# Graph attention and a transformer block: the first groups' work and the last groups' projection in another order

## The chip, the cores and the metric

The kernel runs on one core of a Trainium2 chip. The metric is device time in microseconds (us) of one execution, the median of several runs; lower is better. The engines have short names here: PE is TensorE's matrix multiply, PEld its weight load, DVE VectorE, ACT ScalarE, POOL GpSimd, and SP SyncE, which here only issues transfers (DMAs). Each engine works through its own list of instructions in order and waits for the others by semaphores.

## The reference

There are 64 batches of 64 tokens with 256 features, all float32. A graph attention comes first, then a transformer block with conditioning (cond) by batch:

```python
# graph attention, on x (B, N, F) = (64, 64, 256), with kv the first 20 tokens
q_exp = where(x.sum(-1) == 0, 0, cond)            # by row
self_feat = concat([x, q_exp]) @ W_self.T + b_self
output = self_feat
for d in range(2):
    A = (adj if d == 0 else swapaxes(adj, 1, 2))[:, :, :20, :]      # 11 labels
    mask, label_bias = A.sum(-1) > 0, A @ w_bias + b_bias
    aff = einsum('bnhd,bmhd->bnhm', q, k) / sqrt(16)                # 16 heads
    w = softmax(where(mask, aff, NEG) + label_bias)
    output = output + einsum(w, kv) through Wout + bout
x = x + relu(output)
# transformer block
shift, scale, gate (twice) = split(silu(cond) @ Wt + bt, 6)
h = layernorm(x) * g1 + be1;  h = h * (1 + scale_msa) + shift_msa
x = x + gate_msa * (attention(h) @ Wproj + bproj)
h = layernorm(x) * g2 + be2;  h = h * (1 + scale_mlp) + shift_mlp
x = x + gate_mlp * (gelu(h @ W1 + b1) @ W2 + b2)
```

## The kernel before

**Groups and tiles.** The batches go in nine groups, NB = [4, 8, 8, 8, 8, 8, 8, 8, 4] (L26). A group of 8 is 512 tokens, four tiles of 128 tokens (two batches a tile); the first and the last group have two tiles. Features lie on the partitions (xT, sfT, hT: 128 x 2 x tokens), so that the weights are the stationary operand and 512 tokens stream past them.

**The order is written by hand** (`tc.manual_schedule()`, L71): every engine's list is in the order of the calls in the source. `start()` (L945) does group 0's graph attention, most of group 1's, and the first two slots; then a loop over g = 1 to 7 runs `boundary(g)` and `period(g)`; `finish()` (L1059) does the rest. In period g, the transformer attention of group g, the graph attention of group g+1 and the MLP of group g-1 go side by side. A `slot` (L723) takes one tile of each: scores on PE, then the softmax on DVE, ACT and POOL, transposes back on PE, and the output products. Places named "p", "f0", "f1", "d0", "f2", "f2b", "d1", "d2", "f3" in the slot take further calls from lists of fills, chiefly to give PE work while a softmax is under way.

**PSUM.** Four banks rotate (`bank`, L89); one can be held for a long sum. Two pairs of banks, pa and pb, take the scores. A call that takes a bank waits until whoever read the bank's last content is done.

**Steps of the graph attention.** `graph_k` (L395, keys kT, with wk), `graph_keys` (L425, keys spread by head into kblk; on POOL, for group 1 on ACT in four instructions), `graph_q` (L412, with wq), `graph_scores` (L443), `graph_masked` (L461, DVE times keep, POOL plus term), `graph_exp` (L472: maximum and difference on DVE, exponential on ACT), `graph_normal` (L479: sum and reciprocal on DVE, product w<-w,sm on POOL), `graph_turned` (L486, transposes pwT, ACT copies wT), `graph_output` (L498, po; then ACT, and POOL adds to xT). keep and term come from the adjacency in seven steps (`mask_step`, L334, DVE), six that read it and a last one. `nonzero_rows` (L271) and `row_pairs` (L292) prepare the test for zero rows (pz).

**Steps of the block.** `norm_tokens` (L524, transposes pxT, ACT copies xn), `norm_stats` (L533, DVE statistics and POOL power rstd), `normed` (L544, DVE), `modulated` (L552, transposes phT, DVE times amp, POOL plus off). `half_normed` (L845) is these four as steps 0 to 3 for the first two tiles. Then `block_qk` (pqk), `block_keys` (kb, POOL), `block_scores`, `block_exp` (DVE, ACT), `block_normal` (DVE, POOL), `block_turned` (ppT), `block_attended` (pao), and `block_proj` (L676): four matmuls over the whole group, DVE adds the bias and multiplies by the gate, POOL adds to xT. The MLP is `mlp_up` (pu; Gelu on ACT), `mlp_down` (py), `mlp_gated`, `mlp_out` (store).

**Time projections** (L236) make gate, amp and off from silu(cond): t = 0 to 5, shift, scale and gate for either half; `time_added` (L247) evacuates them on DVE. amp2 and off2 need t = 3 and 4, gate 2 and 5.

**Loads.** SP issues nearly all loads; the first are, in order, xT of group 0, w_self, adj and adj_t of group 0 (L143), wk[0] and wk[1] (L144), then xT of group 1, wout and the rest. ACT issues cond, the other half of w_self, vecs and wq; POOL some broadcasts. `graph_k(0, d)` needs wk[d] and kv; the masks of group 0 need adj and adj_t.

**The end.** `finish()` has E3 (the last tile of group 7, called m), E0 and E1 (the two tiles of group 8, z), the MLP's second half of group 6 (l), the projection and second normalising of m (K[0], K[1]: two tiles each), and the MLPs of m and z. `block_proj(m, c)` needs all four tiles of m attended.

Of the kernel before, what the change touches and what calls it, by code (L numbers as in the profile page):

```python
# [9 lines left out]
F32 = mybir.dt.float32  # L10
I32 = mybir.dt.int32
AF = mybir.ActivationFunctionType
ALU = mybir.AluOpType
# [4 lines left out]
P = 128  # L18
# [28 lines left out]
def graph_attention_then_dit_block(  # L47
# [33 lines left out]
    def unit(name):  # L81

        return gp.tile([P, 512], F32, tag="u", name=name, bufs=8)
# [35 lines left out]
    def load_adj(g):  # L119
        G = groups[g]  # L120
        G.adj = []
        for src in (adj[ds(G.t0, G.T), 0 : M * L], adj_t[ds(G.t0, G.T), :]):
            if g == 0:
                a_d = unit("a_0")[:, 0 : G.nt * M * L].bitcast(I32).rearrange("p (j c) -> p j c", j=G.nt)
            else:
                a_d = two.tile([P, NT, M * L], I32, tag="a_d", name="a_d")[:, 0 : G.nt]
            nc.sync.dma_start(a_d, src.rearrange("(j p) c -> p j c", p=P))
            G.adj.append(a_d)

    def load_w(name, src, k, n, eng):  # L130
        t = wpool.tile([P, k, n], F32, tag=name, name=name)
        eng.dma_start(t, src.rearrange("(k p) n -> p k n", p=P))
        return t
# [8 lines left out]
    w_self_sb = load_w("w_self", w_self[0:D], 2, D, nc.sync)  # L142
    load_adj(0)  # L143
    wk_sb = [load_w(f"wk{d}", wk[d], 2, D, nc.sync) for d in range(2)]  # L144
# [89 lines left out]
    pt_of = {}  # L234

# [440 lines left out]
    def block_proj(g, c):  # L676
        G = groups[g]
        py = bank("pproj")[:, 0 : G.T]
        for k in range(2):
            nc.tensor.matmul(py, wproj_sb[:, k, ts(c, P)], G.aoT[:, k, 0 : G.T], start=(k == 0), stop=(k == 1))  # L680
        if c == 0:
            G.yT = []
        yT = two.tile([P, GT], F32, tag="tq", name="yT") if g == NG - 1 else unit("yT")
        G.yT.append(yT[:, 0 : G.T])
        gated(G.yT[c], py, "bproj", 0, g, c)
        nc.gpsimd.tensor_tensor(G.xT[:, c, :], G.xT[:, c, :], G.yT[c], ALU.add)

# [35 lines left out]
    def slot(e, c, e_next, c_next, before, fill):  # L723
# [4 lines left out]
        C = graph_scores(*c, sc) if c else None  # L728
        if Eb:
            block_turned(Eb)  # L730
        elif Cb:
            graph_turned(Cb[0])
# [137 lines left out]
    def period(g):  # L870
# [4 lines left out]
        def up(*ms):  # L875
            return [(mlp_up, m, i) for i in ms]
# [60 lines left out]
        if n == NG - 1:  # L937

            fills = fills[:3]
            fills[2]["f3"] = up(6) + next_(half_normed, 0) + up(7) + next_(half_normed, 1)  # L940
# [4 lines left out]
    def start():  # L945
# [71 lines left out]
        for t in t1:  # L1017
            graph_masked(t)
        graph_v(1, 0)
# [3 lines left out]
        block_keys(0, 0)  # L1023
        graph_v_spread(1)
# [7 lines left out]
        graph_keys(1, 2)  # L1032
        graph_exp(t1[0])
# [3 lines left out]
        row_pairs(2)  # L1037
        fills = [
            {
                "f0": [(nonzero_rows, 2)],  # L1040
# [6 lines left out]
                    (time_projection, 2), (half_normed, 1, 0), (mask_step, 2, 3), (time_projection, 3),  # L1047
# [5 lines left out]
                "d0": [(half_normed, 1, 2)],  # L1053
                "f3": [(time_projection, 4), (half_normed, 1, 3), (time_projection, 5)],
# [4 lines left out]
    def finish(before):  # L1059

        z, m, l = NG - 1, NG - 2, NG - 3
        Z, A = groups[z], groups[m]
        E3 = block_scores(m, 3, [pair("pa", "sca"), pair("pb", "scb")])
        block_turned(before[0])
        block_exp(E3)
        mlp_down(l, 0, 6, 7)
        half_normed(z, 2)
        block_attended(before[0], pair("pa", "pao")[:, 0])
        mlp_gated(l, 0)
        mlp_out(l, 0)  # L1070
        mlp_down(l, 1, 0)
        half_normed(z, 3)
        block_normal(E3)
        mlp_down(l, 1, 1, 2)
# [3 lines left out]
        mlp_down(l, 1, 3)  # L1078
        block_turned(E3)
        block_qk(z, 0, 0)  # L1080
        block_qk(z, 0, 1)
        block_keys(z, 1)
        block_attended(E3, bank("pao"))
        E0 = block_scores(z, 0, [pair("pa", "sca"), pair("pb", "scb")])
        block_exp(E0)
        block_proj(m, 0)
        block_proj(m, 1)
        block_v(z, 0)
        E1 = block_scores(z, 1, [pair("pa", "sca"), pair("pb", "scb")])
        block_exp(E1)  # L1090
        mlp_down(l, 1, 4)
        K = [Tile() for _ in range(A.nt // 2)]
        norm_tokens(K[0], A.xT, 0)
        norm_stats(K[0])
        mlp_down(l, 1, 5)
        norm_tokens(K[1], A.xT, 1)
        block_normal(E0)
        norm_stats(K[1])
        normed(K[0])
        mlp_down(l, 1, 6)  # L1100
        A.h2T = gp.tile([P, 2, GT], F32, tag="h2b", name="h2T")
        modulated(K[0], A.h2T, 0, amp2, off2, m)
        block_turned(E0)
        normed(K[1])
        block_normal(E1)
        mlp_down(l, 1, 7)
        block_attended(E0, pair("pa", "pao")[:, 0])
        modulated(K[1], A.h2T, 1, amp2, off2, m)
        mlp_gated(l, 1)
        mlp_out(l, 1)  # L1110
        mlp_up(m, 0)
        block_turned(E1)
        mlp_up(m, 1)
        block_attended(E1, pair("pb", "pao")[:, 0])
        block_proj(z, 0)
        block_proj(z, 1)
        mlp_up(m, 2)
        mlp_down(m, 0, 0)
        k = Tile()
        mlp_up(m, 3)  # L1120
        norm_tokens(k, Z.xT, 0)
        norm_stats(k)
        for i in range(4, 6):
            mlp_up(m, i)
            mlp_down(m, 0, i - 3)
        normed(k)
        Z.h2T = new_hT("hT")
        mlp_up(m, 6)
        mlp_down(m, 0, 3)
        modulated(k, Z.h2T, 0, amp2, off2, z)  # L1130
        mlp_up(m, 7)
        mlp_down(m, 0, *range(4, 8))
# [80 lines left out]
```

## Time and profile before

| | us |
|---|---|
| median of 3 runs (708.24, 708.87, 710.34) | 708.87 |
| the profiled execution itself | 706.65 |
| its span, first to last instruction | 704.9 |
| PE busy | 666.8 |
| DVE busy | 494.0 |
| POOL busy | 373.8 |
| ACT busy | 353.8 |

The mean clock granted to PE was 0.985. The costliest groups are the two MLP products, py (L705) with 121.6 us in 288 records and pu (L695) with 109.3 in 256; a float32 matmul shows as two records. Among the others, the average POOL product of `block_normal` (128x1024) takes 1.90 us, that of `graph_normal` 1.36, and the DVE difference of `graph_exp` (L476) 1.60.

The page has the busy time of the engines, then the span in 40 slices of 17.6 us with the busy share in tenths, the chain of work that ended last, and groups by line. Waits are listed as "who line <- whom: us in total, times, longest". A timeline line has the start, the duration, the engine, line and operation, the shape and how many follow each other, and in brackets how long the engine had been idle and what ended that.

### The profile page before, as it was taken

The page shows a single profiled execution, that of the slowest core. Times are in us where ns is not written, and L with a number is a line of the kernel's source. Part 1 is how long each engine was busy: PE and PEld are TensorE (multiplying, and loading weights), DVE is VectorE, ACT ScalarE, POOL GpSimd, SP SyncE. Part 2 cuts the span into 40 slices and gives each one's busy share as a digit, 9 for nine tenths or more (in the row PEclk, how much of TensorE's full clock was granted, in tenths as well). Part 3 has the DMA queues.
Part 4 walks back from the last instruction along what each step waited for, and adds up shares of the span by engine and source line. Part 5 has one row for each costly group of instructions (what it writes and reads, how often), then busy time and mean ns, then how long its engine had stood idle before and what let it go on. Part 6 is the DMA issues. An engine that isn't in the chain of part 4 may idle for free.

```text
span 704.9 us, 15418 instructions
## 1 busy us (share of the span) xinstructions
PE 666.8 (95%) x6414; PEld 408.8 (58%) x6414; DVE 494.0 (70%) x847; ACT 353.8 (50%) x627; POOL 373.8 (53%) x372
## 2 busy tenths in 40 slices
PE   6997889899999999999999999999999999996897
PEld 6664655676655655555655655555655656464446
DVE  3688866789777867887787967887777867557111
ACT  2345333773367435754377535654377537653312
POOL 5545335764676546844575546844665565444310
PEclk8998999999999999999999999999999999998999
DMA  8425040003100040003100040003000100000000
GB/s 282 137 70 185 2 132 18 17 23 95 50 16 17 20 145 17 1 32 103 47 17 16 21 146 16 2 31 93 3 8 12 37 4 2 2 16 1 16 15 31
DMA packets 34382, 33.42 MB, mean 47 GB/s; under 512 B 5608, under 2 KB 28200, under 8 KB 34312
## 3 DMA queue, kind: packets, MB, share of 16 engines
q1 hardware_dynamic: 32808, 31.22, 14.0%
q8 instruction: 51, 0.84, 0.6%
q10 hardware_dynamic: 1232, 0.88, 0.4%
q0 software_dynamic: 272, 0.33, 0.2%
q14 instruction: 19, 0.16, 0.1%
HBM read 25.59 MB, written 6.83 MB: 46 GB/s over the span
## 4 chain that ended last, share of the span: by engine, by line
PE 81%; DVE 10%; ACT 4%; POOL 2%; DMA 2%; issue 1%; ACTq 0%; POOLq 0%; DVEq 0%
PE pu L695 14%; PE py L705 14%; PE pqT L418 8%; PE pqk L576 7%; PE ppT L644 4%; PE pv L584 4%; PE pwT L492 3%; PE pproj L680 3%; PE pf L320 3%; PE pk L403 3%; PE po L510 2%; PE pv L367 2%; PE pao L655 2%; PE sca L614 2%; PE phT L556 2%; PE pxT L529 2%
## 5 line engine op out<-in xcount | busy, mean ns | idle before, releaser
L705 PE MATMUL py<-u,w 128*128 128x512 f32 (+1 forms) x288 | 121.6, 552 | 0.2 <-ACT u L697 0.2
L695 PE MATMUL pu<-h2T,w 128*128 128x512 f32 (+1 forms) x256 | 109.3, 570 | 3.1 <-POOL h2T L563 2.5
L470 POOL TENSOR_TENSOR w<-w,term 128x640 f32<-128x640 f32 x32 | 49.4, 1547 | 72.2 <-DVE w L465 40.2
L695 PEld LDWEIGHTS pu<-h2T,w 128*128 128x128 f32 x256 | 47.4, 190 | 50.1 <-issue 43.1
L705 PEld LDWEIGHTS py<-u,w 128*128 128x128 f32 x288 | 51.2, 191 | 37.7 <-issue 34.4
L637 POOL TENSOR_TENSOR pr<-pr,sm 128x1024 f32<-128x1024 f32 x32 | 60.9, 1902 | 23.0 <-DVE sm L636 20.5
L477 ACT ACTIVATE w<-w 128x640 f32<-128x640 f32 x32 | 23.5, 736 | 87.1 <-DVE w L476 87.1
L521 POOL TENSOR_TENSOR xT<-xT,sfT 128x256 f32<-128x256 f32 x32 | 23.8, 743 | 79.1 <-ACT sfT L520 53.8
L418 PE MATMUL pqT<-sfT,wq 128*128 128x512 f32 (+1 forms) x144 | 61.7, 557 | 0.0
L576 PE MATMUL pqk<-hT,wqkv 128*128 128x512 f32 (+1 forms) x144 | 59.7, 552 | 0.7 <-POOL hT L563 0.6
L697 ACT ACTIVATE u<-pu,vec 128x512 f32<-128x512 f32 (+1 forms) x72 | 42.9, 640 | 34.1 <-PE pu L695 33.2
L484 POOL TENSOR_TENSOR w<-w,sm 128x640 f32<-128x640 f32 x32 | 43.4, 1360 | 29.1 <-DVE sm L483 29.1
L625 DVE TENSOR_REDUCE mx<-sca 128x8 f32<-128x512 f32 x32 | 22.0, 688 | 52.0 <-PE sca L454 43.8
L538 DVE BATCH_NORM_STATS2 st<-xn 128x6 f32<-128x256 f32 x64 | 26.1, 408 | 39.8 <-ACT xn L531 39.8
L635 DVE TENSOR_REDUCE sm<-pr 128x16 f32<-128x1024 f32 x32 | 38.9, 1216 | 20.9 <-ACT pr L631 19.9
L542 POOL TENSOR_TENSOR rstd<-rstd,mhalf 128x2 f32<-128x2 f32 x32 | 23.4, 731 | 55.1 <-DVE rstd L541 54.4
L476 DVE TENSOR_TENSOR w<-w,mx 128x640 f32<-128x640 f32 x32 | 51.2, 1601 | 1.1
L419 ACT ACTIVATE qT<-pqT,vec 128x512 f32<-128x512 f32 (+1 forms) x36 | 23.0, 640 | 52.2 <-PE pqT L418 52.2
L647 ACT COPY pT<-ppT 128x512 f32<-128x512 f32 x64 | 34.5, 591 | 28.8 <-PE ppT L644 28.8
L577 ACT ACTIVATE qk<-pqk,vec 128x512 f32<-128x512 f32 (+1 forms) x36 | 23.1, 640 | 47.3 <-PE pqk L576 47.3
L631 ACT ACTIVATE pr<-pr 128x1024 f32<-128x1024 f32 x32 | 33.8, 1057 | 25.7 <-DVE pr L627 25.5
L547 DVE TENSOR_SCALAR xn<-xn,mv,rstd 128x256 f32<-128x256 f32 x64 | 40.1, 668 | 5.2 <-POOL rstd L542 5.2
(140 smaller groups left out, 1439.2 us busy)
## 6 DMA issues: line engine op xcount, KB each, us to landing
xT<-in_x_t SPq DMA_DIRECT2D x7, 512.0 KB
out<-xT SPq DMA_DIRECT2D x14, 256.0 KB
a_d<-in_adj SPq DMA_DIRECT2D x7, 440.0 KB
a_d<-in_adj_t SPq DMA_DIRECT2D x7, 440.0 KB
x_g<-in_x SPq DMA_DIRECT2D x5, 512.0 KB
vblk<-vd SPq DMA_DIRECT2D x28, 80.0 KB
w<-in_w SPq DMA_DIRECT2D x2, 1024.0 KB
vd<-v_sb SPq DMA_DIRECT2D x7, 256.0 KB
```

The costliest lines, as they stand in the source:

```text
L418: nc.tensor.matmul(pq, wq_sb[d][:, k, ts(c, P)], G.sfT[:, k, :], start=(k == 0), stop=(k == 1))
L470: nc.gpsimd.tensor_tensor(t.w, t.w, G.term[:, :, j, :].unsqueeze(1).to_broadcast([P, H, 2, M]), ALU.add)
L476: nc.vector.tensor_tensor(wf, wf, mx.unsqueeze(2).to_broadcast([P, 2 * H, M]), ALU.subtract)
L484: nc.gpsimd.tensor_tensor(wf, wf, sm.unsqueeze(2).to_broadcast([P, 2 * H, M]), ALU.mult)
L547: nc.vector.tensor_scalar(key.xn[:, i, :], key.xn[:, i, :], key.mv[:, i, 0:1], key.rstd[:, i : i + 1], ALU.subtract, ALU.mult,)
L576: nc.tensor.matmul(pp, wqkv_sb[:, k, ds(i * D + c * P, P)], G.hT[:, k, 0 : G.T], start=(k == 0), stop=(k == 1))
L635: nc.vector.tensor_reduce(sm, t.pr, AX.X, ALU.add)
L637: nc.gpsimd.tensor_tensor(t.pr, t.pr, sm.unsqueeze(2).to_broadcast([P, H, N]), ALU.mult)
L647: nc.scalar.copy(t.pT[:, ts(q4, 4), :], pt.rearrange("p (i t) -> p i t", i=4))
L695: nc.tensor.matmul(pu, w1_sb[:, k, ts(m, P)], G.h2T[:, k, 0 : G.T], start=(k == 0), stop=(k == 1))
L697: nc.scalar.activation(G.u[m], pu, AF.Gelu, bias=col("b1", m))
L705: nc.tensor.matmul(G.py, w2_sb[:, m, ts(c, P)], G.u[m], start=(m == 0), stop=(m == 7))
```

## The change

It touches the two ends of the program and leaves `boundary` as it is; of the periods only the last one's third slot changes.

At the start:
- wk[0] and wk[1] are loaded ahead of group 0's adjacency.
- The keys of group 1's third tile (`graph_keys(1, 2)`) are issued right after the masks of its first two, ahead of ACT's four qk evacuations; the first exponential stands between two and two of these, the second behind them.
- `row_pairs(2)` stands ahead of the two `graph_normal`.
- A new place "p2" in `slot`, behind the scores and ahead of the transposes, takes time projection 2, which was in the first slot's "f3".
- In the second slot, step 2 of `half_normed(1)` moves from "d0" to "d1"; time projection 4 moves behind step 3, and its evacuation behind that of time projection 5.

At the end a new `pair_proj(g, j2)` projects two tiles (256 tokens): eight matmuls of four 128x128 blocks into one bank, two DVE instructions, one POOL add. It replaces both calls of `block_proj` for m (as two pairs) and for z (as one). The first pair of m goes into the third slot of the last period, ahead of up(7). In `finish`, the normalising of K[0] is spread ahead of E3's output, K[1]'s follows the second pair's projection, three up products of m stand before E1's transposes.

```diff
     w_self_sb = load_w("w_self", w_self[0:D], 2, D, nc.sync)
+    wk_sb = [load_w(f"wk{d}", wk[d], 2, D, nc.sync) for d in range(2)]
     load_adj(0)
-    wk_sb = [load_w(f"wk{d}", wk[d], 2, D, nc.sync) for d in range(2)]
...
+    def time_product(t):
+        time_projection(t, bank("pt"))
...
-        yT = two.tile([P, GT], F32, tag="tq", name="yT") if g == NG - 1 else unit("yT")
-        G.yT.append(yT[:, 0 : G.T])
+        G.yT.append(unit("yT")[:, 0 : G.T])
...
+    def pair_proj(g, j2):
+
+        G = groups[g]
+        py = bank("pproj").rearrange("p (c t) -> p c t", c=2)
+        t2 = ts(j2, 2 * P)
+        for c in range(2):
+            for k in range(2):
+                nc.tensor.matmul(
+                    py[:, c], wproj_sb[:, k, ts(c, P)], G.aoT[:, k, t2], start=(k == 0), stop=(k == 1)
+                )
+        y = two.tile([P, GT], F32, tag="tq", name="y").rearrange("p (c t) -> p c t", c=2)
+        b4 = ds(G.b0 + 4 * j2, 4)
+        for c in range(2):
+            nc.vector.scalar_tensor_tensor(
+                y[:, c].rearrange("p (b n) -> p b n", n=N), py[:, c].rearrange("p (b n) -> p b n", n=N),
+                col("bproj", c), gate[:, c, b4].unsqueeze(2).to_broadcast([P, 4, N]), ALU.add, ALU.mult,
+            )
+        nc.gpsimd.tensor_tensor(G.xT[:, :, t2], G.xT[:, :, t2], y, ALU.add)
...
         C = graph_scores(*c, sc) if c else None
+        fill("p2")
         if Eb:
...
-            fills[2]["f3"] = up(6) + next_(half_normed, 0) + up(7) + next_(half_normed, 1)
+            fills[2]["f3"] = up(6) + next_(half_normed, 0) + [(pair_proj, g, 0)] + up(7) + next_(half_normed, 1)
...
             graph_masked(t)
+        graph_keys(1, 2)
         graph_v(1, 0)
         graph_v(1, 1)
         block_qk(0, 1, 0)
         block_qk(0, 1, 1)
         block_keys(0, 0)
+        graph_exp(t1[0])
         graph_v_spread(1)
...
         block_qk(0, 0, 0)
         block_qk(0, 0, 1)
-        graph_keys(1, 2)
-        graph_exp(t1[0])
+        row_pairs(2)
         graph_exp(t1[1])
         graph_normal(t1[0])
         graph_normal(t1[1])
-        row_pairs(2)
         fills = [
             {
+                "p2": [(time_projection, 2)],
...
-                    (time_projection, 2), (half_normed, 1, 0), (mask_step, 2, 3), (time_projection, 3),
+                    (half_normed, 1, 0), (mask_step, 2, 3), (time_projection, 3),
...
-                "d0": [(half_normed, 1, 2)],
-                "f3": [(time_projection, 4), (half_normed, 1, 3), (time_projection, 5)],
+                "d1": [(half_normed, 1, 2)],
+                "f3": [(half_normed, 1, 3), (time_product, 4), (time_projection, 5), (time_added, 4)],
```

`finish` after the change, from its beginning to the last `modulated`; the rest is as before:

```python
E3 = block_scores(m, 3, [pair("pa", "sca"), pair("pb", "scb")])
block_turned(before[0]); half_normed(z, 2); block_exp(E3); mlp_down(l, 0, 6, 7)
block_attended(before[0], pair("pa", "pao")[:, 0]); mlp_gated(l, 0); mlp_out(l, 0)
half_normed(z, 3); norm_tokens(K[0], A.xT, 0); mlp_down(l, 1, 0)
block_normal(E3); norm_stats(K[0]); mlp_down(l, 1, 1)
block_qk(z, 1, 0); block_qk(z, 1, 1); block_keys(z, 0); mlp_down(l, 1, 2)
block_turned(E3); block_qk(z, 0, 0); block_qk(z, 0, 1)
normed(K[0]); block_keys(z, 1); modulated(K[0], A.h2T, 0, amp2, off2, m)
block_attended(E3, bank("pao"))
E0 = block_scores(z, 0, [pair("pa", "sca"), pair("pb", "scb")])
block_exp(E0); mlp_down(l, 1, 3); pair_proj(m, 1); block_v(z, 0); block_normal(E0)
E1 = block_scores(z, 1, [pair("pa", "sca"), pair("pb", "scb")])
mlp_down(l, 1, 4); norm_tokens(K[1], A.xT, 1); norm_stats(K[1]); mlp_down(l, 1, 5, 6)
normed(K[1]); block_turned(E0); modulated(K[1], A.h2T, 1, amp2, off2, m)
block_exp(E1); mlp_down(l, 1, 7); block_attended(E0, bank("pao"))
mlp_gated(l, 1); mlp_out(l, 1); mlp_up(m, 0); block_normal(E1); mlp_up(m, 1); mlp_up(m, 2)
block_turned(E1); mlp_down(m, 0, 0); mlp_up(m, 3)
block_attended(E1, pair("pb", "pao")[:, 0]); mlp_down(m, 0, 1); pair_proj(z, 0)
mlp_up(m, 4); mlp_down(m, 0, 2); mlp_up(m, 5); norm_tokens(K[2], Z.xT, 0); norm_stats(K[2])
mlp_down(m, 0, 3); mlp_up(m, 6); normed(K[2]); mlp_down(m, 0, 4); mlp_up(m, 7)
modulated(K[2], Z.h2T, 0, amp2, off2, z)
```

More of the change, by code (lines that the diff above doesn't have):

```diff
@@ L1062, in finish @@
         Z, A = groups[z], groups[m]
+        K = [Tile() for _ in range(3)]
+        A.h2T = gp.tile([P, 2, GT], F32, tag="h2b", name="h2T")
         E3 = block_scores(m, 3, [pair("pa", "sca"), pair("pb", "scb")])
         block_turned(before[0])
+        half_normed(z, 2)
         block_exp(E3)
         mlp_down(l, 0, 6, 7)
-        half_normed(z, 2)
         block_attended(before[0], pair("pa", "pao")[:, 0])
@@ L1070, in finish @@
         mlp_out(l, 0)
+        half_normed(z, 3)
+        norm_tokens(K[0], A.xT, 0)
         mlp_down(l, 1, 0)
-        half_normed(z, 3)
         block_normal(E3)
-        mlp_down(l, 1, 1, 2)
+        norm_stats(K[0])
+        mlp_down(l, 1, 1)
         block_qk(z, 1, 0)
@@ L1077, in finish @@
         block_keys(z, 0)
-        mlp_down(l, 1, 3)
+        mlp_down(l, 1, 2)
         block_turned(E3)
@@ L1081, in finish @@
         block_qk(z, 0, 1)
+        normed(K[0])
         block_keys(z, 1)
+        modulated(K[0], A.h2T, 0, amp2, off2, m)
         block_attended(E3, bank("pao"))
@@ L1085, in finish @@
         block_exp(E0)
-        block_proj(m, 0)
-        block_proj(m, 1)
+        mlp_down(l, 1, 3)
+        pair_proj(m, 1)
         block_v(z, 0)
+        block_normal(E0)
         E1 = block_scores(z, 1, [pair("pa", "sca"), pair("pb", "scb")])
-        block_exp(E1)
[L1091 to L1105, printed above, removed]
+        mlp_down(l, 1, 4)
+        norm_tokens(K[1], A.xT, 1)
+        norm_stats(K[1])
+        mlp_down(l, 1, 5, 6)
+        normed(K[1])
+        block_turned(E0)
+        modulated(K[1], A.h2T, 1, amp2, off2, m)
+        block_exp(E1)
         mlp_down(l, 1, 7)
-        block_attended(E0, pair("pa", "pao")[:, 0])
-        modulated(K[1], A.h2T, 1, amp2, off2, m)
+        block_attended(E0, bank("pao"))
         mlp_gated(l, 1)
@@ L1111, in finish @@
         mlp_up(m, 0)
+        block_normal(E1)
+        mlp_up(m, 1)
+        mlp_up(m, 2)
         block_turned(E1)
-        mlp_up(m, 1)
+        mlp_down(m, 0, 0)
+        mlp_up(m, 3)
         block_attended(E1, pair("pb", "pao")[:, 0])
[L1115 to L1126, printed above, removed]
-        Z.h2T = new_hT("hT")
[L1128 to L1132, printed above, removed]
+        mlp_down(m, 0, 1)
+        pair_proj(z, 0)
+        mlp_up(m, 4)
+        mlp_down(m, 0, 2)
+        mlp_up(m, 5)
+        norm_tokens(K[2], Z.xT, 0)
+        norm_stats(K[2])
+        mlp_down(m, 0, 3)
+        mlp_up(m, 6)
+        normed(K[2])
+        mlp_down(m, 0, 4)
+        mlp_up(m, 7)
+        Z.h2T = new_hT("hT")
+        modulated(K[2], Z.h2T, 0, amp2, off2, z)
+        mlp_down(m, 0, 5, 6, 7)
         mlp_gated(m, 0)
```

## The prediction

> **What bounds the kernel now.** I read the page first, then the waits of TensorE, its timeline round the longest ones, one-microsecond windows there for the clock, and last the ScalarE timeline at 51 to 62 us. Page and waits:
>
> ```profile
> PE 666.8 (95%) x6414; PEld 408.8 (58%) x6414; DVE 494.0 (70%) x847; ACT 353.8 (50%) x627; POOL 373.8 (53%) x372
> ...
> PE   6997889899999999999999999999999999996897
> ...
> PEclk8998999999999999999999999999999999998999
> ```
>
> ```profile
> PE phT L556 <- DVE xn L547: 8.9, 6, 6.0
> PE pk L403 <- DMA wk<-in_wk: 4.6, 1, 4.6
> PE pwT L492 <- POOL w L484: 3.3, 2, 2.5
> PE pu L695 <- POOL h2T L563: 2.5, 1, 2.5
> ...
> PE ppT L644 <- DVE hT L559: 2.0, 1, 2.0
> ```
>
> TensorE is the bound: 666.8 of 704.9 us busy, so 38 us without work, and the slices put that at the two ends (slices 1 to 8 and 37 to 40). The middle, periods 1 to 6, which the change doesn't touch, has 9s. The waits name the holes, the timeline dates them:
>
> ```profile
> 13.13 3.67 PE L403 MATMUL pk<-kv,wk 128*128 128x80 f32 x16 [4.57 <-DMA wk<-in_wk]
> ```
>
> ```profile
> 646.32 1.14 PE L556 MATMUL phT<-ident,xn 128*128 128x128 f32 x4 [6.01 <-DVE xn L547]
> 647.25 1.91 PE L644 MATMUL ppT<-ident,pr 128*128 128x128 f32 x8
> ...
> 654.09 1.98 PE L695 MATMUL pu<-h2T,w 128*128 128x512 f32 x4 [2.55 <-POOL h2T L563]
> ```
>
> The windows add a second cost. Columns: stretch, its length, busy us of PE, PEld, DVE, ACT, POOL, then the granted clock, DMA share and GB/s.
>
> ```profile
> 12.00:13.00 1.00, 0.00 (x0) 0.00 (x0) 0.93 (x3) 0.00 (x0) 0.00 (x0) 0.50 1.06 386
> ```
>
> ```profile
> 60.00:61.00 1.00, 0.23 (x2) 0.00 (x0) 1.00 (x4) 0.73 (x2) 1.00 (x1) 0.50 0.94 365
> ...
> 65.00:66.00 1.00, 1.00 (x2) 0.45 (x2) 1.00 (x1) 0.00 (x0) 0.63 (x1) 0.50 0.05 17
> 66.00:67.00 1.00, 1.00 (x16) 0.61 (x17) 0.84 (x2) 0.59 (x1) 0.00 (x0) 0.97 0.00 0
> ```
>
> After each long hole the clock is half: from 11.4 to 18.3, 59.2 to 66.1 and 642.9 to 649.7, 6.8 us each. Half of TensorE's busy time inside is lost where TensorE is the bound: 2.6 (13.13 to 18.3), up to 2.9 (5.86 busy) and 1.7 us (646.3 to 649.7). The hole at 56.2 to 58.6 comes from ScalarE's order:
>
> ```profile
> 54.03 1.37 ACT L432 ACTIVATE kblk<-kT,hmask 128x160 f32<-128x160 f32 x4
> 55.30 1.35 ACT L477 ACTIVATE w<-w 128x640 f32<-128x640 f32 x2
> ```
>
> The two exponentials of group 1 stand behind four projections and the third tile's keys, and behind them come sums, reciprocals (DVE to 58.3) and the two normalisings (POOL, from 57.41).
>
> [...] the drops lie 14 and 171 windows of 3.413 us apart. One window with 1.0 us of work dropped, one with 1.6 (90.0 to 93.4) did not, one with 2.45 stayed at half. [...] L476 takes 0.83 to 2.02 us here[...]. [...] Here adj landed by 8.3, adj_t at 11.5 and wk[0] at 13.0 us.
>
> **Part 1, wk ahead of the adjacency (SP).** Four transfers swap; bytes, lane waits and everything behind stay. wk[0] takes adj's place (262 KB for 225), so it should land before 9.4; wk[1] takes adj_t's, 11.5 to 12.0. Then pk waits for kv (POOL, 10.87) and starts at 10.9 instead of 13.13: 2.2. pk and pqT took 7.95 us, partly at half clock. At full clock they are 2.0 + 3.45 us (16 records of 0.215, half a row of L418), with about 0.25 for wk[1]; wq landed at 12.0 and 13.4 by what SP's issues waited for, in time. That saves 2.25. Scores start at 16.6 for 21.05: 4.4. Cover: adj_t now lands where wk[1] did, by 15.0 (pk ran through then). Three mask steps of 0.61 and 0.7 for keep and term end at 17.6; scores end at 17.9. Each us later than 15.3 would cost one. No absolute arrival binds behind it: wt, wqkv and xT are in by 22 us.
>
> **Part 2, keys, exponentials and first time projection.** The third keys need only kT and a free kblk (scores of tile 0, 46.7), so ScalarE does them at 47.2 to 48.6, where it was idle to 51.07. Exponential 0 fits between the projections at 52.4, exponential 1 at 54.1. Sums run from 53.8 for 56.06, the normalised tile 0 is there at 56.2 for 58.7; row_pairs (1.27) moves ahead on POOL into 53.1 to 54.4, where it was idle. PE has 0.84 us of the time projection in between, so the hole of 2.4, the 0.96 before pz and the half clock go. What is late next is DVE, then ScalarE's FIFO: the exponential of tile 2 (64.2 to 65.0) stands ahead of wT of tile 1, so PE comes early, pauses about 3.0 us at 63 to 66, and reaches the second slot's scores at 71.9 for 75.5. Saved: 3.5.
>
> **Part 3, second slot.** The normalising of xn (2.28 us on DVE, beside POOL) moves behind v_sb, hT ahead of amp and off, and both time projections behind phT. By the rows the chain to ppT is 1.0 shorter: rstd and sums 83.0, mx and w 85.2, v_sb 85.8, xn 86.7, phT and 2 x 0.85 of projection, pk and pv 90.7 for 91.77, in before's frame. But PE now pauses 83.4 to 86.3. Worth between -1 (worse) and +1.5; I take 1.0.
>
> Parts 1 to 3: 4.4 + 3.5 + 1.0 = 8.9. Three pauses are new or left: 2.2, 3.0 and 2.9 us. Each may drop the clock: bounds 0 and 3.4 (two windows at half). At 1.7, one window[...], 2.3 is expected; I take 2.0 off: **6.9**.
>
> **Part 4, the end.** block_proj(m) was 8 records of 512 (3.63 us), pair_proj is 2 x 1.73; DVE's y goes from 2 x 0.74 to 4 x 0.48, POOL's adds stay 2 x 1.27. For z, matmuls and y stay, POOL's two adds of 0.8 become one of 1.27. The first pair's projection, before up(7), pushes scores E3 back by 1.7. E3's exponential gets 2.5 later, since y, statistics and xn stand before it on DVE, and hT 1.3 later behind POOL's y2T add (ready 625.3). PE has phT, pxT and two downs meanwhile and waits 0.4 there, 0.3 before ppT(E3). Then K0 needs no wait: its xn is done at 629.5, long before PE gets to phT at 630.8. E0's scores come at 631.9 for 630.0, the second projection ends at 635.2, value and E1 scores at 637.6, downs and ppT(E0) at 641.7, phT(K1) 642.5 (xn 642.2), last down and pao 644.0, and up(0) starts when POOL adds off2 at 644.3. Before, that was 654.09, with the same matmuls done. Check: holes 6.01 + 2.55, half clock 1.7 and 0.2 of projection are 10.5, less new waits of about 0.9: 9.6, near the 9.8. Behind it up(1), up(2) cover ppT(E1) but 0.7 (before 0.5, in front of pproj). K2 is hidden by ups in both. DVE against POOL may cost 0.5: **9.3**.
>
> **Sum.** 6.9 + 9.3 = 16.2 off the profiled execution's 706.65 (span 704.9 and 1.75 round it) is 690.45. That execution lies 2.2 below the runs' median of 708.87, so I predict 692.7.
>
> **Rivals.**
> A, the start gives most of its gain back: the new pauses all drop the clock for two windows (10.2 instead of 2.0), so parts 1 to 3 end at -1.3. For it: 59.2 to 66.1 stayed half at 72% busy. Against: behind the pauses PE is full, so one window should do, and that is 8.9 - 5.1 = 3.8, 695.8. Whole: 700.9; midway, 698.3.
> B, the end's wait moves rather than goes: POOL has pr(E3), rstd, four kb and off2 in one FIFO, and a slip of its 1.9 us pr pushes K0, then E0 and K1. For it: POOL 3.9 of 5 us busy in 650 to 655. Against: a slack of 1.3 at phT(K0). Half the end's gain: 697.3.
> C, slower: [...] Two long holes are traded for many short pauses. If each drops the clock at 3.4 us, 18.7 gross (8.9 + 9.8) is eaten by 5.5 drops; from there on it decides, and 6.5 give 712.3. I count three pauses over 2 us.
> D, nothing changes because the starts and ends are bound elsewhere: 708.9. Against: the chain of waits runs through these very holes.
>
> **Numbers.** Forecast 0.66, A 0.15, B 0.10, C 0.05, D 0.04. Own range of the forecast, from no drop to two whole ones and a slip of 1: 689 to 697; with half of A, and B, 688.5 to 699.5. About 0.3% (2.1 us) is what this kernel's measurement can tell from none: faster 0.91, same 0.04, slower 0.05.
>
> **What would show it.** pk's wait of 4.57 becomes about 2.2, for POOL's kv; no half clock at 12 to 18 in most runs; pwT without a wait on POOL; a new PE pause before po's second tile, on ScalarE; phT's 6.01 and pu's 2.55 gone, up(0) of the last but one group at 654.09 less 9.8 and 6.9, near 637. Wrong would be: adj_t later than 15.3, pauses over 2 us after 620, or middle periods of another length.

## The result, and the profile after

The changed kernel takes 697.11 us in the median of four runs (696.66 to 698.78). The kernel before took 709.61 beside it: 12.5 us less, a ratio of 0.983 with an interval of 0.980 to 0.986. A second set beside other runs gave 697.97 against 709.57, 0.984 (0.981 to 0.987). The time lies 0.1 us above the forecast's own range (689 to 697), inside the wider one (688.5 to 699.5), and nearer to what rival B (697.3) and rival A in half (698.3) named than to 692.7, so it takes the traces to tell these apart. The gain is about three quarters of the 16.2 us that the sum gave by the medians, and six tenths of it between the two profiled executions. One execution of a later run, at 842.32 us and a clock of 0.753 where that run's five others had 0.990 to 0.995, is left out of its numbers.

The profiled execution of the changed kernel took 696.66 us (span 695.0), 9.99 less than that of before. The positions below compare these two executions. Lines of the code stand 3 higher than before from `time_product` to `block_proj`, and 21 or 22 higher behind `pair_proj`. From the page after, TensorE's busy time, its slices and its clock:

```profile
PE 667.1 (96%) x6422; PEld 412.2 (59%) x6422; DVE 493.1 (71%) x849; ACT 353.2 (51%) x627; POOL 374.8 (54%) x371
...
PE   8998799899999999999999999999999999899997
...
PEclk9999889999999999999999999999999999999999
```

TensorE's busy time is what it was, and the span without work fell from 38.1 to 27.9 us. Slice 1 has 8 for 6 and slice 37 has 9 for 6, but slice 5 has 7 for 8, and the clock's two 8s stand in slices 5 and 6. TensorE's waits after (who, on whom: us in total, times, longest):

```profile
PE phT L559 <- DVE xn L550: 5.6, 5, 3.5
PE po L509 <- ACT sfT L520: 3.3, 1, 3.3
PE ppT L647 <- ACT u L718: 2.6, 2, 1.6
PE pk L406 <- POOL kv L331: 2.0, 1, 2.0
...
PE phT L559 <- ACT pT L650: 0.8, 1, 0.8
...
PE pu L716 <- POOL h2T L566: 0.5, 1, 0.5
```

The wait for wk is gone and pk waits 2.0 for kv, the 6.0 of phT at the end is gone and pu's 2.5 is down to 0.5, in the main as forecast. New are a 3.3 before po and a 3.5 before phT, both near the start. The timeline of TensorE dates them:

```profile
10.70 2.69 PE L406 MATMUL pk<-kv,wk 128*128 128x80 f32 x16 [1.97 <-POOL kv L331]
...
17.80 0.51 PE L457 MATMUL sca<-kblk,qT 64*64 64x80 f32 x16
...
62.51 0.75 PE L509 MATMUL po<-sfT,ident 128*128 128x128 f32 x4 [3.27 <-ACT sfT L520]
63.19 1.09 PE L513 MATMUL po<-wT,vblk 80*32 80x64 f32 x32
64.21 3.09 PE L323 MATMUL pf<-xT,w_self 128*128 128x512 f32 x4
...
70.86 0.51 PE L457 MATMUL sca<-kblk,qT 64*64 64x80 f32 x16
...
81.62 1.13 PE L559 MATMUL phT<-ident,xn 128*128 128x128 f32 x4 [3.48 <-DVE xn L550]
82.55 3.52 PE L245 MATMUL pt<-siluT,wt_sb 128*128 128x64 f32 x16
85.85 2.45 PE L406 MATMUL pk<-kv,wk 128*128 128x160 f32 x8
88.23 1.08 PE L381 MATMUL pv<-wout,kv 128*32 128x128 f32 x16
89.24 1.62 PE L647 MATMUL ppT<-ident,pr 128*128 128x128 f32 x8
```

Short stretches (from and to, length, busy us of PE, PEld, DVE, ACT, POOL, granted clock, DMA share, GB/s) show what each pause brought:

```profile
65.00:66.00 1.00, 1.00 (x2) 0.34 (x1) 0.77 (x1) 0.00 (x0) 1.00 (x1) 0.50 0.00 0
...
85.00:86.00 1.00, 1.00 (x6) 1.00 (x7) 0.00 (x0) 0.00 (x0) 0.33 (x1) 0.50 0.00 0
```

In the clock records of the two traces every stretch of half or full clock between two changes is a whole multiple of 3.413 us (before: half for 6.83 three times, full for 40.96 and 576.85 between them, 12 and 169 multiples); a window, here, is one such 3.413 us. After the change the clock was half from 11.9 for one window, from 63.0 for one, and from 80.1 to 90.4 for three, 10.24 us, although TensorE's records are busy without a gap from 81.62. The end has two small waits in the place of the two large ones:

```profile
610.06 1.99 PE L716 MATMUL pu<-h2T,w 128*128 128x512 f32 x4
...
641.14 0.78 PE L559 MATMUL phT<-ident,xn 128*128 128x128 f32 x4 [0.81 <-ACT pT L650]
643.83 5.42 PE L716 MATMUL pu<-h2T,w 128*128 128x512 f32 x12 [0.46 <-POOL h2T L566]
```

Four lines of before, for the landmarks:

```profile
21.02 0.51 PE L454 MATMUL sca<-kblk,qT 64*64 64x80 f32 x16
...
76.09 0.51 PE L454 MATMUL sca<-kblk,qT 64*64 64x80 f32 x16
...
91.77 1.07 PE L644 MATMUL ppT<-ident,pr 128*128 128x128 f32 x8 [2.01 <-DVE hT L559]
...
612.42 1.98 PE L695 MATMUL pu<-h2T,w 128*128 128x512 f32 x4
```

The landmarks of both traces, us from the start of the span:

| landmark | before | after | gain so far |
|---|---|---|---|
| keys of group 0 (pk) | 13.13 | 10.70 | 2.4 |
| scores of group 0 | 21.02 | 17.80 | 3.2 |
| first transposes (pwT) | 31.23 | 28.02 | 3.2 |
| graph scores of the second slot | 76.09 | 70.86 | 5.2 |
| ppT of the first boundary | 91.77 | 89.24 | 2.5 |
| up(6) of the last period | 612.42 | 610.06 | 2.4 |
| up(0) of group 7 in the finish | 654.09 | 643.83 | 10.3 |

So the start gains 5.2 and gives 2.7 back in its second slot, and the end brings 7.9 to up(0), 7.6 to the end of the span.

### The profile page after: what moved, and what is told of

It reads as the page before. It is cut to its first block, busy times and chain, and to the rows that moved or that the text cites. A ratio compares the mean times of both kernels' runs of the same rounds, so it can differ in the third digit from the quotient of the medians.

```text
span 695.0 us, 15433 instructions
## 1 busy us (share of the span) xinstructions
PE 667.1 (96%) x6422; PEld 412.2 (59%) x6422; DVE 493.1 (71%) x849; ACT 353.2 (51%) x627; POOL 374.8 (54%) x371
## 3 DMA queue, kind: packets, MB, share of 16 engines
HBM read 25.59 MB, written 6.83 MB: 47 GB/s over the span
## 4 chain that ended last, share of the span: by engine, by line
PE 81%; DVE 9%; POOL 3%; ACT 3%; DMA 2%; issue 1%; POOLq 0%; ACTq 0%; SPq 0%
PE py L726 14%; PE pu L716 14%; PE pqT L421 7%; PE pqk L579 7%; PE ppT L647 4%; PE pv L587 4%; PE pwT L495 3%; PE pf L323 3%; PE pk L406 3%; PE po L513 3%; PE pproj L683 2%; PE pv L370 2%; PE pao L658 2%; PE phT L559 2%; PE sca L617 2%; PE pxT L532 2%
## 5 line engine op out<-in xcount | busy, mean ns | idle before, releaser
L487 POOL TENSOR_TENSOR w<-w,sm 128x640 f32<-128x640 f32 x32 | 43.3, 1357 | 24.1 <-DVE sm L486 23.9
L634 ACT ACTIVATE pr<-pr 128x1024 f32<-128x1024 f32 x32 | 33.8, 1057 | 29.3 <-DVE pr L630 29.1
L550 DVE TENSOR_SCALAR xn<-xn,mv,rstd 128x256 f32<-128x256 f32 x64 | 38.5, 641 | 7.7 <-POOL rstd L545 7.7
```

What stands on the lines that cost most here:

```text
L487: nc.gpsimd.tensor_tensor(wf, wf, sm.unsqueeze(2).to_broadcast([P, 2 * H, M]), ALU.mult)
L550: nc.vector.tensor_scalar(key.xn[:, i, :], key.xn[:, i, :], key.mv[:, i, 0:1], key.rstd[:, i : i + 1], ALU.subtract, ALU.mult,)
```

## The experiments

Single executions of one kernel differ by several us (27 of the kernel before beside the first four runs: 705.52 to 711.47), so small differences are read from landmarks, and times as ratios to the runs of before.

**The end alone, and the start alone.** The first is the kernel before with `pair_proj`, the last period's third slot and `finish` of the change; the second is the changed kernel with those three as before.

> The kernel before with the change's end alone: projection in pairs of tiles, the first pair's in the third slot of the last period, the new order of the finish; the start is that of before. Theory (read from the two traces): the end gave 7.6 us of the 10.0 between the two profiled executions, so this kernel is 7 to 8.5 us faster than before, about 701.5 to 702.5, and the first 600 us of its trace agree with before. Rival (the end by hand, 9.8 us, was right, and the start lost something on the way that the traces hide): 9.5 to 10 us faster.

> The change with the end of before. Theory: the start alone is worth 2 to 4.5 us (2.0 to 2.4 between the two profiled executions; the medians differ by 2.5 us more than the profiles, and the variable part of a run is its clock windows in the start), so 705 to 707.5. Rival (the start is as large as predicted, 6.9 us, and the profiled execution of before merely had luck at its start): 702 to 703.

The end alone took 699.94 us, ratio 0.989 (0.986 to 0.992): 7.7 us by the ratio, 8.9 by the two medians, and the interval reaches to 9.9, so the times alone don't rule out the rival's 9.5. The trace does: its span is 697.7 and its scores of group 0 come 0.45 later than in before, which makes 7.6, and from up(6) of the last period to the end of the span it is 84.9 us for 92.5. The theory was met by the trace, the 9.8 by hand was not reached. The start alone took 705.71 in 22 executions, 0.996 (0.995 to 0.998): 2.7 us. The start is not as large as predicted and hidden by a lucky profile of before: the rival's 702 to 703 is out. By the ratios the two parts come to 10.4 us together, near the 10.0 between the profiles.

**The loads alone.** One line of the change on the kernel before:

```diff
+    wk_sb = [load_w(f"wk{d}", wk[d], 2, D, nc.sync) for d in range(2)]
     load_adj(0)
-    wk_sb = [load_w(f"wk{d}", wk[d], 2, D, nc.sync) for d in range(2)]
```

> The kernel before with the change's first line alone: the keys' weights loaded ahead of the first group's adjacency. Theory (the first scores of TensorE start 16.2 to 19.7 us into the span in the ten profiled executions with this order and at 21.0 and 21.5 in the two without it, by where the clock's window falls, and what is gained there stays): 2.5 to 4 us faster than before, so that this line is worth all that the start is worth, and the other two parts cancel each other. Rival (the later start of the second group's features, which wait for a load, gives the early gain back): 0 to 1.5 us faster, and the gain of the start came from the other two parts.

It took 706.35 in 22 executions against 708.70, 0.996 (0.994 to 0.998): 2.4 to 2.8 us, at the low end of the theory and as much as the whole start. Parts 2 and 3 together are worth about nothing.

Why it stops there shows in the trace of the start alone, where the clock did not fall at 12 us. Two stretches of its TensorE timeline, and then VectorE's:

```profile
12.56 3.66 PE L421 MATMUL pqT<-sfT,wq 128*128 128x256 f32 x16
...
28.04 1.07 PE L495 MATMUL pwT<-ident,w 128*80 128x128 f32 x8 [2.08 <-POOL w L487]
```

```profile
12.79 0.61 DVE L346 TENSOR_REDUCE cnt<-a 128x40 f32<-128x440 int32 x1 [2.62 <-DMA a<-in_adj]
13.43 1.68 DVE L349 TENSOR_TENSOR a<-a,wb 128x440 f32<-128x440 int32 x1
...
16.31 1.62 DVE L349 TENSOR_TENSOR a<-a,wb 128x440 f32<-128x440 int32 x1
...
18.96 0.30 DVE L359 SCALAR_TENSOR_TENSOR term<-vb,bb,term 128x80 f32<-128x80 f32 x1
19.18 0.48 DVE L468 TENSOR_TENSOR w<-sca,keep 128x320 f32<-128x320 f32 x1
```

The scores come at 16.15 there, 1.65 earlier than in the changed kernel's profile, and pwT starts at the same time (28.04 for 28.02): it waits 2.08 for POOL in the place of 0.76. VectorE gets the first adjacency at 12.79 and is through with the masks at 19.2, since two of its products take 1.68 and 1.62 us in the place of 0.62. What is late next, once wk is early, is the adjacency that it was moved ahead of. The changed kernel's profile, with its slower scores, has the other case:

```profile
19.15 0.49 DVE L468 TENSOR_TENSOR w<-sca,keep 128x320 f32<-128x320 f32 x1 [0.36 <-PE sca L457]
```

All fourteen profiles, of before and after and of the twelve runs, fit one account: from this first masking to pwT it is 8.86 or 8.87 us, and the masking starts 1.35 us after the first scores or, where the masks are later, as they end. In the four with full clock at the first scores (16.15 to 16.5) the masks set it, at 18.4 to 19.2; in the others the scores do.

**Part 3 taken back.** The second slot's fills as before, in the changed kernel:

```diff
-                "d1": [(half_normed, 1, 2)],
-                "f3": [(half_normed, 1, 3), (time_product, 4), (time_projection, 5), (time_added, 4)],
+                "d0": [(half_normed, 1, 2)],
+                "f3": [(time_projection, 4), (half_normed, 1, 3), (time_projection, 5)],
```

> The changed kernel with its third part taken back: the normalised half stands ahead of the exponential again and time projections 4 and 5 have their old order around the turned halves. Theory (part 3 turned a saving of 1.0 into a loss of 3 us through three windows of half clock): 2.5 to 3.5 us faster than the changed kernel, about 694, with full clock at 81 to 91 us. Rival (the pause that follows from part 2 is there whatever the order of part 3, and so is its clock): 0 to 1.5 us slower than the changed kernel, with half clock at the same place.

695.97 us, 0.982 (0.980 to 0.985); against the changed kernel's 0.983 and 0.984 that is a lean of one us, and the intervals overlap. In the traces the way from the second slot's graph scores to ppT is 15.7 us without part 3, as in before, and 18.4 with it: its cost of 2.7 is there. The clock stayed full at 80 to 86. But a wait took its place, two lines on TensorE:

```profile
79.51 0.55 PE L559 MATMUL phT<-ident,xn 128*128 128x128 f32 x3 [0.78 <-DVE xn L550]
...
85.95 1.11 PE L647 MATMUL ppT<-ident,pr 128*128 128x128 f32 x8 [2.00 <-DVE hT L562]
```

After this 2.0 the clock fell (86.8 to 90.2), behind the landmark, which took 1.1 of the 2.7 back by the scores of period 1. Where the spell falls moved with the pauses; "full clock at 81 to 91" was missed.

**Both time products ahead of the turned halves.** One line in the second slot:

```diff
-                "f3": [(half_normed, 1, 3), (time_product, 4), (time_projection, 5), (time_added, 4)],
+                "f3": [(time_product, 4), (time_product, 5), (half_normed, 1, 3), (time_added, 4), (time_added, 5)],
```

> The changed kernel with both remaining time products issued ahead of the turned halves in the second slot of the first period, so that the 3.5 us pause of TensorE at 78 to 82 us has their 16 small matmuls inside it. Theory (a pause long enough costs a spell of half clock, and the spell cost more than the pause): the pause shrinks to about 1.8 us, no half clock follows at 81 to 91 us, and the time falls by 3 to 5 us against the changed kernel, to about 692.5 to 694. Rival (the clock falls since small weight-bound matmuls do not count as work, and these are now themselves in the critical window): half clock is still there for two or more windows, and the gain is 0 to 1.8 us, the time moved alone.

694.63 us, 0.981 (0.978 to 0.983): by the ratios 1.6 to 2.6 us below the changed kernel's two sets, and the intervals overlap. In the trace the way from the second slot's graph scores to ppT is 15.3 us for 18.4, 3.0 less. That is the lower end of the theory's size, and its reason was half wrong: the pause shrank to 1.55 us, and half clock followed all the same, as the rival had said, for two windows (82.84 to 89.67) and not three. The window before it, in full clock:

```profile
79.43:82.84 3.41, 2.78 (x50) 2.47 (x48) 3.34 (x5) 0.06 (x1) 1.90 (x1) 1.00 0.00 0
```

TensorE's records fill 2.78 of 3.41 us, 81%, and the clock fell at its end. Of its 50 records, 48 stream only 64 columns. Whether busy records alone set the clock had to be tested by itself.

**The changed kernel again, and its pauses filled.** Matmuls that nothing reads, into unused columns of the output pair; nothing of the computation is left out:

```diff
+    def wide(n):
+        for _ in range(n):
+            nc.tensor.matmul(last_po[0][:, 1, D : 2 * D], ones, wqkv_sb[:, 0, 0:D], start=True, stop=True, skip_group_check=True)
...
-                "f3": [(half_normed, 1, 3), (time_product, 4), (time_projection, 5), (time_added, 4)],
+                "f3": [(wide, 10), (half_normed, 1, 3), (time_product, 4), (time_projection, 5), (time_added, 4)],
```

> The changed kernel itself once more, as the base for the runs beside it. It should be 697 us within 1.5, 1.6 to 1.8% under before. Where the pauses of 3.3 us near 60 us and 3.5 us near 78 us decide the clock, both are followed by half clock here again, though the edges of the spells may lie elsewhere.

> The changed kernel with 10 matmuls of 256 columns that nothing reads, written to unused columns of the output pair, ahead of the turned halves of the second slot, so that TensorE has 3 us of wide work in the pause at 78 to 81.6 us. Theory (the pause sets the clock): no half clock at 80 to 91 us, the product of the time projections takes 1.8 instead of 3.5 us and the keys 1.25 instead of 2.45, and the time falls by 2.5 to 4 us against the changed kernel. Rival (the long run of small matmuls behind the pause, 64 and 160 columns, does not count as work): half clock begins all the same, at 83 to 88 us, and the time is within 1 us of the changed kernel.

> The same, and 9 such matmuls more in the pause at 59 to 62.5 us, between the turning and the output of the first slot's second tile. Theory: no half clock at 63 to 67 us either, the self product there takes 1.9 us instead of 3.1, and the time is 1 to 2 us below the run with the second pause alone filled, 4 to 5.5 us below the changed kernel. Rival (the clock spell there is hidden, since VectorE sets the next wait): the same as with the second pause alone, within 0.5 us.

The changed kernel: 697.97, with both spells of half clock again. One pause filled: 700.52, 0.988 (0.984 to 0.992). Both filled: 704.17, 0.994 (0.991 to 0.996). Slower by 2.6 and 6.2 us, and neither theory is tested as meant. TensorE's timeline with one filled says why:

```profile
83.03 6.77 PE L748 MATMUL po<-wqkv,ones 128*128 128x256 f32 x20 [4.07 <-ACT sfT L520]
89.63 0.60 PE L559 MATMUL phT<-ident,xn 128*128 128x128 f32 x4
90.07 1.90 PE L245 MATMUL pt<-siluT,wt_sb 128*128 128x64 f32 x16
91.80 1.31 PE L406 MATMUL pk<-kv,wk 128*128 128x160 f32 x8
```

The added work waited 4.07 us for ScalarE's reading of the pair, though in other columns, and so began behind the pause; whether the chip asks for that wait or only the program's semaphores do, no run shows. But it answers another question. The clock fell at 80.65 and was back at 87.48, two windows later, with 256 columns from 83.03 on. In the changed kernel, with 64 and 160 columns from 82.55 on, it took three (80.12 to 90.36). And pt and pk took 1.90 and 1.31 us at full clock, for 3.52 and 2.45.

**What a small matmul counts for.** Two probes. The first puts stretches that nothing reads at the head of three middle periods:

```diff
+        for at, count, cols in ((3, 96, 64), (4, 76, 160), (5, 24, 512)):
+            if g == at:
+                dm = bank("dm")
+                for _ in range(count):
+                    nc.tensor.matmul(dm[:, 0:cols], ones, wqkv_sb[:, 0, 0:cols], start=True, stop=True)
```

> A probe, longer by its added work: the changed kernel with 96 matmuls of 64 columns at the head of the period of group 3, 76 of 160 columns in that of group 4, and 24 of 512 columns in that of group 5, each about 12 to 14 us of back-to-back work that nothing reads. If small matmuls do not count as work for the clock, the stretch of 64 columns falls to half clock within its first two windows (7 us) and that of 512 stays full; the stretch of 160 columns says where the limit lies. If only pauses count, all three stay at full clock from end to end, at 0.125, 0.156 and 0.59 us for one matmul.

The second is the run with one pause filled, with `(wide, 10)` as 30 matmuls of 64 columns.

> A probe, longer by its added work: as the run that filled the second pause, whose wide matmuls turned out to start behind the pause and not in it, but with 30 matmuls of 64 columns (60 records) in the place of its 10 of 256 (20 records). There the clock fell near 80.7 us and came back near 87.5, two windows of 3.41 us on, with wide work from 83 us. Theory (a stretch of 64 columns at full clock kept it, 21 us long, but does not win it back once it is half): the whole stretch runs at half clock, 0.22 us a record, 13 us, and full clock returns only in the wide work after it, four or more windows after the drop. Rival (any back-to-back stretch brings it back at the end of the first whole window): full clock returns at 87.5 us again, and the stretch takes about 9 us.

The first probe's stretches of 64, 160 and 512 columns in TensorE's timeline, and the clock in the first:

```profile
266.99 21.55 PE L916 MATMUL dm<-wqkv,ones 128*128 128x64 f32 x192
...
367.44 20.81 PE L916 MATMUL dm<-wqkv,ones 128*128 128x160 f32 x152
...
467.18 20.76 PE L916 MATMUL dm<-wqkv,ones 128*128 128x512 f32 x48
```

```profile
278.00:282.00 4.00, 4.00 (x38) 4.00 (x38) 0.00 (x0) 0.00 (x0) 0.00 (x0) 1.00 0.23 48
```

All three stay at full clock (1.00 in each 4 us inside them), the small ones for 21.55 us, six windows. (The run took 759.79 us, the second probe 713.00, one execution each. Each matmul shows as two records, of 0.112, 0.137 and 0.433 us by number of columns, so the stretches are twice the 12 to 14 us that I expected.) The second probe, TensorE and one us of the clock:

```profile
84.76 13.06 PE L748 MATMUL po<-wqkv,ones 128*128 128x64 f32 x60 [4.08 <-ACT sfT L520]
97.61 1.06 PE L559 MATMUL phT<-ident,xn 128*128 128x128 f32 x4
98.47 3.52 PE L245 MATMUL pt<-siluT,wt_sb 128*128 128x64 f32 x16
```

```profile
95.00:96.00 1.00, 1.00 (x7) 1.00 (x6) 0.00 (x0) 0.00 (x0) 0.00 (x0) 0.50 0.00 0
```

All 13.06 us ran at half clock, 0.218 us a record for the 0.112 of the first probe, and full clock came back at 106.95, seven windows after the fall at 83.05 (the wide run: two). So the theory holds and its rival is out: in these two runs back-to-back matmuls of 64 columns keep a full clock, and don't win it back. Here and in the changed kernel the window at whose end it came back (103.53 to 106.95; 86.95 to 90.36) held records of 160 and 128 columns alone, and half or more of the one before it went to 64. By the first probe a record of 512 columns takes 0.4325 us; at the same rate, 64 columns would stream in 0.054 of the 0.112 us that one takes, 48%. That is an estimate, and that the streamed columns are what counts is not shown. But 64 columns kept full clock for 21.55 us where it was full, and half for 13.06 us where it was half: in these two runs it took more to come back than to stay. Before's windows point the same way, though their shares are of records and not of columns: one with 1.6 of 3.41 us (47%) didn't fall and one with 2.45 (72%) didn't come back.

**The first pair's projection later.** Out of the third slot, into `finish` behind `block_exp(E3)`:

> The changed kernel with the first pair's projection taken out of the third slot and put into the finish, behind the exponential of the last period's last tile. Theory (the third slot is what brings the first pair's residual, and so the first half's tokens, in time): VectorE adds the gated pair behind that exponential, at about 621 us, GpSimd's sum ends at about 623, and TensorE waits 1.5 us for it at the tokens of the first half; 1 to 2.5 us slower than the changed kernel. Rival (the pairing alone gives the gain, the slot has slack): within 0.5 us of the changed kernel.

697.93 us, 0.983 (0.980 to 0.986): the same as the changed kernel, as far as an interval of 4 us tells. TensorE:

```profile
619.68 1.89 PE L697 MATMUL pproj<-aoT,wproj 128*128 128x256 f32 x8
...
625.08 0.66 PE L532 MATMUL pxT<-ident,xT 128*128 128x128 f32 x4 [0.62 <-POOL xT L707]
...
647.12 3.27 PE L716 MATMUL pu<-h2T,w 128*128 128x512 f32 x7 [0.46 <-POOL h2T L566]
```

From up(6) of the last period to up(0) it takes 33.07 us, with the third slot 33.77. The tokens wait 0.62 for POOL as the theory said (it had 1.5), but the wait of 0.70 before E3's products goes, since VectorE reaches E3's exponential earlier. The rival is right: the pairs and the new order of `finish` bring the gain, the place in the third slot doesn't. Which of those two, no run separated.

**Real work in both pauses.** `self_product(2, 1)` stands between the transposes and the output of the first slot's second tile, and both time products are first:

```diff
             if i > 0:
                 graph_turned(t)
+            if i > 0:
+                fill("fm")
             graph_output(t, po[:, i])
...
+                "fm": [(self_product, 2, 1)],
                 "d1": [(self_features, 2, 0), (self_cond, 2, 1)],
...
-                    (self_product, 2, 1), (mask_step, 2, 1), (block_v, 0, 0), (self_features, 2, 1), (mask_step, 2, 2),
+                    (mask_step, 2, 1), (block_v, 0, 0), (self_features, 2, 1), (mask_step, 2, 2),
...
-                "f3": [(half_normed, 1, 3), (time_product, 4), (time_projection, 5), (time_added, 4)],
+                "f3": [(time_product, 4), (time_product, 5), (half_normed, 1, 3), (time_added, 4), (time_added, 5)],
```

> A version that may beat the changed kernel: real work in both pauses. The self product of the second half of group 2 stands between the turning and the output of the first slot's second tile (1.9 us of wide work in the pause of 3.3 us near 60 us), and both time products stand ahead of the turned halves in the second slot, as in the run that put the products first. Theory (TensorE's empty time there is on the path): the second slot's scores come 1.5 to 2 us earlier than in the changed kernel even where the clock falls, 3 where it doesn't, and with the 2.5 us that the products first gave the time is 3.5 to 5.5 us below the changed kernel, 692.5 to 694.5. Rival (VectorE sets what follows, and filling TensorE's pause earlier only moves it): no better than with the products first alone, 694 to 695.5.

693.56 us in the median of five executions (691.42 to 695.39), 0.977 (0.974 to 0.980), the lowest of all. By the ratios that is 4 to 5 us below the changed kernel's two sets, and 2.6 below the run with the products first, where the intervals overlap. It lies in the theory's range, but less than half a us under the rival's, so the time doesn't decide. TensorE near 60 us, and at ppT:

```profile
62.72 1.98 PE L323 MATMUL pf<-xT,w_self 128*128 128x512 f32 x4 [2.84 <-DVE sfT L330]
64.54 0.61 PE L509 MATMUL po<-sfT,ident 128*128 128x128 f32 x4
...
84.93 1.69 PE L647 MATMUL ppT<-ident,pr 128*128 128x128 f32 x8 [1.76 <-DVE gate L257]
```

The product itself waited 2.84 us, for a bank that VectorE still read, so the pause stayed; but po followed it without a wait. The clock stayed full here, pf took 1.98 us for 3.09, and from the first slot's scores to the second's it is 17.5 us for 19.4, where the theory had 3 for this case. Of these 1.9 the rows at full clock explain 1.6. That the clock stayed full looks like luck, by an estimate: seven windows counted back from the fall at 85.2, an edge lies at 61.3, inside the pause, and the windows on its two sides had 1.97 and 2.01 us of records, where the changed kernel's one window of 59.64 to 63.05 had 0.54. Half clock came at 27 and at 85.2 us, for one window each. From the second slot's scores to ppT it is 15.35 us, and 15.34 with the products first, though the clock was full here and half there: in its place ppT waits 1.76 for VectorE's gate. What the moved product does by itself, one profile doesn't say; nor was it run without the products first.

## Why the prediction was right, and where its sum was off

**Right in its steps.** The three holes named (wk, phT, pu) went, the new waits stand where they were put: pk on POOL's kv with 1.97 (forecast 2.2), po's second tile on ScalarE with 3.27 (3.0), phT on VectorE's xn with 3.48 (2.9). pwT of the second group waits for POOL no longer, only the first still does, 0.76 as before. No pause after 620 exceeds 2 us, the middle kept its length (up(6) of the last period less ppT: 520.65 before, 520.82 after). But up(0) came at 643.83, not near 637, so the steps were right and the sizes were not.

**Part 1, 4.4: measured 3.2.** "Scores start at 16.6 for 21.05" came true where the clock was full there (16.15 to 16.5); in the changed kernel's profile it was half for one window, and they start at 17.80. The term that failed is "three mask steps of 0.61 and 0.7 for keep and term end at 17.6": they end at 18.8 in that profile and 19.2 in the start alone, since products of 0.62 took 1.60, 1.62 and 1.68. Before, the changed kernel and the start alone have six such products: the three that began while POOL was at its key spreading or `row_pairs` took 1.60 to 1.68 us, and the three that began before it 0.62. The difference of `graph_exp` (L476) in before's trace leans the same way: 0.82 and 0.83 us in the two that ran while POOL was idle, 0.94 to 2.02 in the 30 that overlap its work. That POOL's work is the cause is not shown, since no run took it away. The masks hide a part of the clock: pwT came at 27.2 to 28.0 where it was full for pk and pqT, at 28.0 to 29.3 with one window at half, at 29.7 and 29.9 with two. So with full clock part 1 is worth 3.2 to 4.0. "No half clock at 12 to 18 in most runs" was wrong: of the twelve profiles with the keys' weights first, eight had some, one of them at 9.3 to 12.7.

**Part 2, 3.5: measured 2.0.** The 1.5 between is the clock at 63.0: po and its products took 1.84 for 1.36, pf 3.09 for 1.98, 1.6 in all.

**Part 3, 1.0: measured -2.7 up to ppT.** From phT to ppT it is 7.62 us, with half clock, and 3.98 in the run with one pause filled, at full clock: the spell cost 3.6, most of it in pt (1.62) and pk (1.14). Without it part 3 would have been worth 0.9 by this landmark. That is an estimate, and a wait on VectorE could have come in its place, as it did with real work in both pauses.

**The clock term, 2.0: measured 5.2.** The 2.0 was the author's estimate, and this is the step that failed. "Behind the pauses PE is full, so one window should do" was true for the pause at 60 us, behind which 512-column products stand, and false for that at 78 us, behind which stand 64 and 160 columns. Rival A had it half: three windows, not two, but after one pause out of three. By size its midway, which leaves the start 2.8, was nearer than the forecast's 6.9: at ppT 2.5 were measured. Without their clock terms (1.6 and 3.6) parts 2 and 3 come out at 3.6 and 0.9, near the 3.5 and 1.0 of the sum, so the gross account was right but for part 1. Before's three spells fit "one window should do": TensorE's records filled the last window of each to within 0.02 us, and full clock followed. Wide work fits it too: with one pause filled, full clock came back at 87.48, at the end of the first window full of 256 columns. Work that is busy by the records alone doesn't: 13.06 us of 64 columns in the second probe, where it took seven windows, and in the changed kernel the window from 83.54 to 86.95, with 3.41 us of records, two thirds of them of 64 columns, and half clock again behind it. And no window ahead of a fall was empty in the changed kernel: TensorE's records filled 1.44, 0.54 and 1.43 us of the three.

**The end, 9.3: measured 7.6.** Shifted by 2.4 for the start, the second projection begins at 634.4 where the sum ended it at 635.2, 0.9 late; phT(K1) at 643.5 for 642.5, with the wait of 0.81 for the bank that ScalarE's pT still held, which the sum had not; up(0) at 646.2 for 644.3, since the chain of phT, VectorE and POOL to it took 2.69 where the sum had 1.8. Rival B, half the gain lost to a moved wait, is not it: no wait there exceeds 0.81.

**The base.** 2.2 was added since the profile of before lay that much below its runs' median; the change's own profile lay only 0.45 below its median. Of the later set of before it lay 2.96 below, and 2.96 less 0.45 is the difference between 12.5 by median and 10.0 by profile. Executions of before differ with their clock (of 27 beside the loads alone, from 705.84 us at 0.987 to 712.82 at 0.973; the middle one has 0.982, the profiled one 0.985), so the median holds half clock that the profile didn't have and the working didn't see. Profile against profile the sum is 6.2 too large, and that the time comes within 4.4 of 692.7 is in part luck.

## What to carry to other kernels

When work is reordered, look at what stands behind each pause that is left: in the run with one pause filled, 256-column matmuls brought the clock back at the end of the first window full of them (at 87.48 us), and in the second probe a run of 64-column ones stayed at half for as long as it lasted (13.06 us). So try the wide product first behind a pause (no run here tested that order by itself). When a load is moved forward, price the one that it passes: its consumer can be the next floor, as the masks were here wherever the clock was full. A place in the order that looks essential by hand (the third slot) can be worth nothing, and a run with that part alone moved tells.

## What the runs showed of the hardware

- Half clock from its start to its end, by what came behind the pause: 256 columns, two windows (6.83 us, 80.65 to 87.48 with one pause filled); 64 and 160 columns, three (10.24 us, 80.12 to 90.36 in the changed kernel); 64 columns for 13.06 us, seven (23.9 us, 83.05 to 106.95 in the second probe). At full clock, 21.55 us of 64-column matmuls never lost it (first probe, 266.99 to 288.5).
- A window whose TensorE records were 81% busy (2.78 of 3.41 us, 48 of 50 records of 64 columns, 79.43 to 82.84 with the products first) was followed by half clock.
- A VectorE product of 128x440 took 0.62 us, and 1.60 to 1.68 where it began while GpSimd was at its own products (before, the changed kernel, the start alone); nothing else was varied to show the cause.
